# Own terms of a two-way scan moved from VectorE to products in PSUM

## Chip, cores and metric

The kernel runs on one core of one Trainium2 chip. The metric is the device time of one execution in microseconds (us). One execution was taken by the hardware profiler; its span lies inside the device time of the same execution. PE is TensorE, DVE is VectorE, ACT is ScalarE, POOL is GpSimd, SP issues the DMAs.

## The reference, cut to what matters

Four layers work on an image batch `x` of 32 x 192 x 56 x 56 in fp32, each as `x = x + layer(group_norm(x))`: an attention, a two-way linear recurrence (RWKV), a small blur of shifted channels, and a long convolution done by a Fourier transform. Only the second is touched:

```python
def wkv_scan(w, u, k, v):                 # along the 3136 pixels of one image
    def step(carry, kv_t):
        p, q, o = carry                   # o: running maximum, for range only
        kt, vt = kv_t
        no = jnp.maximum(o, u + kt)
        A, Bw = jnp.exp(o - no), jnp.exp(u + kt - no)
        y = (A * p + Bw * vt) / (A * q + Bw)
        no2 = jnp.maximum(w + o, kt)
        A2, B2 = jnp.exp(w + o - no2), jnp.exp(kt - no2)
        return ((A2 * p + B2 * vt, A2 * q + B2, no2), y)
...
```

Without the running maximum this says: with ek = exp(k) and bv = ek v, two sums decay by a factor per pixel and take in bv and ek. The output at a pixel is (p + exp(u) bv) / (q + exp(u) ek), where p and q are the sums of the pixels before. "Own term" is exp(u) times the pixel's own value. The layer does this forwards and backwards, adds both, multiplies by a gate sigmoid(r), normalises over the 192 channels, multiplies by a matrix `Wo` and adds the residual. k, v and r are projections of the normalised x by 192 x 192 matrices. The next layer's group norm needs mean and variance of the result, called x2.

## The kernel before, in words

`all_blocks` runs one layer after the other: `make_filter`, `attention`, `scan_pairs` (the second layer), a guarded version of it that runs only if a value went out of range, and `channel_blocks` (the last two layers). They are separate stages of time.

`scan_pairs` takes the 32 images in 16 pairs. The 192 channels of two images fill three tiles of 128 partitions: tile 0 has channels 0 to 127 of the first image, tile 1 those of the second, tile 2 the last 64 channels of both. Pixels go in four chunks (m) of 784, each in two halves of 392, since a PSUM bank holds 512 fp32 values. A PSUM tile, given by `turned()`, is two banks; there are four of them (`bufs=4`), all of PSUM. `_Pairs.outer` makes one 192 x 192 product for tiles 0 and 1, `_Pairs.inner` for tile 2: per chunk 8 products in `outer` (four with the full 128 x 128 weight `aa`, four that take 64 rows, `ca`) and 6 in `inner` (two full `cc`, four with 64 columns, `ac`).

For one chunk:

- `forwards` normalises x on ACT (L1052), makes k and v on PE, ek = exp(k) on ACT (L1101), bv on DVE (L1106). Then for each tile `scan` and `inverse` run, and DVE multiplies (L1113) into `y`.
- `scan` treats bv (name `p`) and ek (name `q`) alike: POOL copies the carry in (L1065), DVE scans (L1070), POOL copies the new carry out (L1071), and DVE adds the own term with one operation, exp(u) x src + before (L1072), where `before` is the scan's result shifted by one pixel. The buffers `pq` are five.
- `inverse` makes 1 / den on ACT as exp(-ln den) (L1077, L1078); the sum that comes with it is kept in `seen` for the range check.
- `backwards` makes the gate g = 1 / (1 + exp(-r)) from PE and ACT (L1126 to L1131), scans the other way, and DVE multiplies (L1134), adds to `y` (L1135) and multiplies by g (L1136).
- `finish` centres over channels (PE, `centre`), squares on ACT (L1149), takes the variance by a product with `mean_w`, and multiplies by `Wo` (`wog`). DVE scales (L1169), adds bias and residual (L1170), and takes x2's sums with two BATCH_NORM_STATS a tile (`stats_of`, L986). SP stores x2.
- `measure` takes the same statistics of a later pair's x, also at L986. `deviations` and `norm` turn the statistics into mean and scale (small products at L1002 and L1003).

The main loop takes pair p's `backwards` from the last chunk to the first; beside it run `finish` of the chunk before, `forwards` of the next pair, and `measure` of the pair after that. Each engine works its queue strictly in order. The order in each queue is set when the program is built: a scheduler moves instructions of independent work past each other, so queues do not follow the source exactly.

Of the kernel before, what the change touches and what calls it, by code (L numbers as in the profile page):

```python
# [876 lines left out]
def scan_pairs(ctx: ExitStack, tc: tile.TileContext, a, k, x1, x2, rs2, wogT, count):  # L877
# [15 lines left out]
    def small(name, shape):  # L893
        return cp.tile(shape, F32, name=name, tag=name)
# [6 lines left out]
        return [t[:, h * HM : (h + 1) * HM] for h in range(2)]  # L901


    wo = [small("wo_a", [128, C]), small("wo_c", [64, C])]
    lg = [small("lg_a", [128, 1]), small("lg_c", [64, 1])]
    lb = [small("lb_a", [128, 1]), small("lb_c", [64, 1])]
    cen = [small("cen_a", [128, C]), small("cen_c", [64, C])]
    for i, r in enumerate((slice(0, 128), slice(128, C))):
        nc.sync.dma_start(out=wo[i], in_=a["L1_conv_WoT"][r])
        nc.sync.dma_start(out=lg[i], in_=a["L1_conv_ln_g"][r].unsqueeze(1))  # L910
# [10 lines left out]
    for i, r in enumerate((slice(0, 128), slice(128, C))):  # L921
        n = (128, 64)[i]
        ps, _, _ = turned()
        for s in range(2):
            nc.tensor.matmul(ps[:n, 0, :C], cen[s][:, r], wo[s], start=(s == 0), stop=(s == 1))
        turn = wp.tile([128, C], F32, name="turn", tag="turn", bufs=1)
        nc.vector.tensor_copy(turn[:n], ps[:n, 0, :C])
        nc.sync.dma_start(out=wogT[r], in_=turn[:n])

    wk, wv, wr = (blocks(n, a[f"L1_conv_{n}T"]) for n in ("Wk", "Wv", "Wr"))  # L930
    wog, centre, mean_w, group = (
# [2 lines left out]
    wd = pairs.vector("wd", a["L1_conv_w_decay"])  # L934
    eu = pairs.vector("eu", a["L1_conv_u"])
    nc.scalar.activation(eu, eu, AF.Exp)

    w = small("w", [128, 2])
    nc.scalar.activation(w, wd, AF.Exp)
# [64 lines left out]
        pairs.inner(group, [ps[:, 1, 2:3]], [[s] for s in src])  # L1004
        return ps[:, :, 1], ps[:, 1, 2:3]

    def deviations(st):

        mv = moments(st)
        first, third = grouped([mv[:, t, 0:1] for t in range(3)])  # L1010
        mean = sp.tile([128, 3], F32, name="mean", tag="mean", bufs=4)
        nc.vector.tensor_copy(mean[:, 0:2], first)
        nc.vector.tensor_copy(mean[:, 2:3], third)
        d = sp.tile([128, 3], F32, name="d", tag="d", bufs=4)
        nc.vector.tensor_tensor(d, mv[:, :, 0], mean, ALU.subtract)
        nc.vector.tensor_tensor(d, d, d, ALU.mult)
        nc.vector.tensor_tensor(d, d, mv[:, :, 1], ALU.add)
        return mean, d
# [20 lines left out]
    class State:  # L1039


        def __init__(self, p, scaling):
            self.p, (_, self.rs, self.nb) = p, scaling
            self.seen = sp.tile([128, 5, 3 * NM], F32, name="seen", tag="seen", bufs=3)
            self.ek, self.bv, self.y = {}, {}, {}
            self.fore, self.back = start("f"), start("b")
            self.st2 = new_stats("st2")

    def normed(s, m):
        xs = load(s.p, m)  # L1050
# [1 line left out]
            nc.scalar.activation(xs[t], xs[t], AF.Identity, bias=s.nb[:, t : t + 1], scale=s.rs[:, t : t + 1])  # L1052
        return [parts(t) for t in xs]

    def scan(s, m, t, carry, rev):

        b, e = s.bv[m][t], s.ek[m][t]
        c = eu[:, of(t)]
        got = []
        for i, src in enumerate((b, e)):  # L1060
            z = wp.tile([128, MC + 1], F32, name="pq"[i], tag="pq", bufs=5)
            edge, last = (MC, 0) if rev else (0, MC)
            out, before = (z[:, 0:MC], z[:, 1:]) if rev else (z[:, 1:], z[:, 0:MC])
            at = carry[t][i]
            nc.gpsimd.tensor_copy(z[:, edge : edge + 1], at)  # L1065
            if rev:
                out, data = out[:, ::-1], src[:, ::-1]
            else:
                data = src[:, :]
            nc.vector.tensor_tensor_scan(out, decay[:, of(t)].to_broadcast([128, MC]), data, at, ALU.mult, ALU.add)  # L1070
            nc.gpsimd.tensor_copy(at, z[:, last : last + 1])  # L1071
            nc.vector.scalar_tensor_tensor(before, src, c, before, ALU.mult, ALU.add)  # L1072
            got.append(before)
        return got

    def inverse(s, den, m, t, which):
        nc.scalar.activation(den, den, AF.Ln)  # L1077
        nc.scalar.activation(den, den, AF.Exp, scale=-1.0, accum_out=s.seen[:, which, 3 * m + t : 3 * m + t + 1])  # L1078

    def start(way):  # L1080
        carry = [[sp.tile([128, 1], F32, name=f"{way}{i}{t}", tag=f"{way}{i}{t}") for i in range(2)] for t in range(3)]
# [5 lines left out]
    def forwards(s, m):  # L1087
        s.ek[m] = [kp.tile([128, MC], F32, name="ek", tag="ek") for _ in range(3)]
        s.bv[m] = [kp.tile([128, MC], F32, name="bv", tag="bv") for _ in range(3)]
        s.y[m] = [kp.tile([128, MC], F32, name="y", tag="y", bufs=3 * NM + 4) for _ in range(3)]  # L1090
        xn = normed(s, m)
        for tiles in ((0, 1), (2,)):
            for wt in (wk, wv):
                ps = [turned() for _ in tiles]
                if len(tiles) == 2:
                    pairs.outer(wt, [q[2] for q in ps], xn)
                else:
                    pairs.inner(wt, ps[0][2], xn)
                for t, (_, both, _) in zip(tiles, ps):
                    if wt is wk:  # L1100
                        nc.scalar.activation(  # L1101
                            s.ek[m][t].rearrange("p (h n) -> p h n", h=2), both, AF.Exp,
                            accum_out=s.seen[:, 0, 3 * m + t : 3 * m + t + 1],
                        )
                    else:
                        nc.vector.tensor_tensor(  # L1106
                            s.bv[m][t].rearrange("p (h n) -> p h n", h=2), both,
                            s.ek[m][t].rearrange("p (h n) -> p h n", h=2), ALU.mult,
                        )
            for t in tiles:  # L1110
                num, den = scan(s, m, t, s.fore, False)
                inverse(s, den, m, t, 1)
                nc.vector.tensor_tensor(s.y[m][t], num, den, ALU.mult)  # L1113

    def backwards(s, m):
        xn = normed(s, m)
        h = s.y[m]
        for tiles in ((0, 1), (2,)):
            ps = [turned() for _ in tiles]
            if len(tiles) == 2:  # L1120
                pairs.outer(wr, [q[2] for q in ps], xn)
            else:
                pairs.inner(wr, ps[0][2], xn)
            for t, (_, both, _) in zip(tiles, ps):
                g = wp.tile([128, MC], F32, name="g", tag="t")
                nc.scalar.activation(  # L1126
                    g.rearrange("p (h n) -> p h n", h=2), both, AF.Exp, scale=-1.0,
                    accum_out=s.seen[:, 3, 3 * m + t : 3 * m + t + 1],
                )
                nc.scalar.activation(g, g, AF.Ln, bias=1.0)  # L1130
                nc.scalar.activation(g, g, AF.Exp, scale=-1.0)  # L1131
                num, den = scan(s, m, t, s.back, True)
                inverse(s, den, m, t, 2)
                nc.vector.tensor_tensor(num, num, den, ALU.mult)  # L1134
                nc.vector.tensor_tensor(h[t], h[t], num, ALU.add)  # L1135
                nc.vector.tensor_tensor(h[t], h[t], g, ALU.mult)  # L1136

    def finish(s, m):
        h, xs = s.y[m], load(s.p, m)
# [19 lines left out]
        for tiles in ((0, 1), (2,)):  # L1159
            po = [turned() for _ in tiles]  # L1160
            if len(tiles) == 2:
                pairs.outer(wog, [q[2] for q in po], hs)
            else:
                pairs.inner(wog, po[0][2], hs)
            for t, (_, out, _) in zip(tiles, po):
                rd = rds[t]
                rdh = rd.rearrange("p (h n) -> p h n", h=2)
                nc.scalar.activation(rd, rd, AF.Exp, scale=-0.5)
                nc.vector.tensor_tensor(rdh, out, rdh, ALU.mult)  # L1169
                nc.vector.scalar_tensor_tensor(xs[t], rd, cb[:, of(t)], xs[t], ALU.add, ALU.add)  # L1170
                stats_of(s.st2, m, t, xs[t])
        rows = slice(m * MC // S, (m + 1) * MC // S)
        for r, t, i, c in places:
            nc.sync.dma_start(out=x2[c, i, rows, s.p], in_=xs[t][r].rearrange("p (h w) -> p h w", w=S))
# [20 lines left out]
        for t, x in enumerate(load(p, m)):  # L1195
            stats_of(st, m, t, x)

    s, after, before = State(0, norm(*deviations(stats_for(0)))), norm(*deviations(stats_for(1))), None
    for m in range(NM):
        forwards(s, m)  # L1200
    for p in range(last):
        ahead = State(p + 1, after) if p + 1 < last else None
        st = new_stats("st1")
        for i in range(NM):
            m = NM - 1 - i
            backwards(s, m)
            if i > 0:
                finish(s, m + 1)
            elif before is not None:
                finish(before, 0)  # L1210
            if ahead is not None:
                forwards(ahead, i)
            if p + 2 < last:
                if i < 2:
                    measure(st, p + 2, 2 * i)
                    measure(st, p + 2, 2 * i + 1)
                elif i == 2:
                    spread = deviations(st)
                else:
                    after = norm(*spread)  # L1220
            if before is not None:
                if i == 1:
                    before.spread = deviations(before.st2)
                elif i == 2:
                    conclude(before)
        before, s = s, ahead
    finish(before, 0)
    before.spread = deviations(before.st2)
    conclude(before)
    nc.sync.dma_start(out=rs2[0:128], in_=kept_a)  # L1230
    for i, r in enumerate((slice(0, 64), slice(64, 128))):
# [580 lines left out]
```

## Time and profile before

Times are in us; three runs.

| what | value |
|---|---|
| median of the runs (lowest, highest) | 12770.67 (12757.16, 12775.48) |
| profiled execution, device time | 12763.6 |
| its span | 12761.8 |
| mean granted PE clock | 0.953 |
| PE busy in the span | 11522.3 (90%) |
| DVE busy | 11221.3 (88%) |
| ACT busy | 5979.7 (47%) |
| POOL busy | 2199.4 (17%) |
| attention: its last products end | 4996 |
| `scan_pairs`: first projection to last small product | 5081.6 to 8828.5 |

A group of the profile is all instructions of one line, operation and pair of tiles: busy time in all, mean length of one, and the time its engine stood idle just before them. The page divides the span in 40 slices of 319 us; a digit is the busy share in tenths. One fp32 product appears as two matmul records. Records of matmuls overlap, since they are pipelined.

### The profile page before, as it was taken

To read this page: it belongs to the slowest core of one execution; us is meant where nothing else is said; L and a number is where in the kernel's file an instruction comes from. 1 tells how busy PE (TensorE), PEld (TensorE's weight loads), DVE (VectorE), ACT (ScalarE), POOL (GpSimd) and SP (SyncE) were. 2 spreads that over 40 slices of the span, in tenths; PEclk is the share of its full clock that TensorE was granted. 3 is DMA by queue.
4 is the path that set the end of the run, shared out by engine and by line. 5 is a ranking of instruction groups with operands and counts; after the bars stand their busy time and mean duration, and the time that the engine had idled before them with its cause. 6 is when DMAs were issued, how large, how long until landed. Compare 5 with 4: busy or idle time off the path is not lost. (4 is left out here: it accounts for less than half of the span.)

```text
span 12761.8 us, 165194 instructions
## 1 busy us (share of the span) xinstructions
PE 11522.3 (90%) x63158; PEld 7190.8 (56%) x63158; DVE 11221.3 (88%) x15929; ACT 5979.7 (47%) x11146; POOL 2199.4 (17%) x2238
## 2 busy tenths in 40 slices
PE   4999999999999997788878788787999999999999
PEld 1556555565555564333333333334777777777777
DVE  3888888888888886999999999998888888888888
ACT  2554554554554553555555555554333333333333
POOL 0000000000000000544445454544000000000000
PEclk8999999999999998889988899898999999999999
DMA  2111111111111112344443344433111111111111
GB/s 64 40 39 39 39 39 49 47 39 39 39 41 53 41 39 68 84 110 103 99 110 97 105 107 103 103 98 81 43 42 44 42 44 44 42 42 44 43 44 28
DMA packets 949574, 770.40 MB, mean 60 GB/s; under 512 B 769870, under 2 KB 811065, under 8 KB 939760
## 3 DMA queue, kind: packets, MB, share of 16 engines
q1 hardware_dynamic: 948776, 759.74, 22.7%
q8 instruction: 504, 8.26, 0.3%
q14 instruction: 294, 2.41, 0.1%
HBM read 479.96 MB, written 240.50 MB: 56 GB/s over the span
## 5 line engine op out<-in xcount | busy, mean ns | idle before, releaser
L589 DVE SCALAR_TENSOR_TENSOR o<-v_a,dww,o 128x896 f32<-128x896 f32 (+1 forms) x1024 | 1053.0, 1028 | 396.5 <-ACT v_a L563 314.2
L1739 ACT COPY y<-ps 64x252 f32<-64x252 f32 (+1 forms) x2376 | 806.4, 339 | 1132.6 <-PE ps L1733 1102.1
L1657 PE MATMUL ps<-f,real 84*84 84x112 f32 x6144 | 1090.8, 259 | 0.0
L1657 PE MATMUL ps<-f,imag 84*84 84x112 f32 x6144 | 1089.4, 259 | 0.0
L1664 ACT COPY z<-ps 84x448 f32<-84x448 f32 x768 | 405.0, 527 | 1219.9 <-PE ps L1657 1218.4
L1657 PEld LDWEIGHTS ps<-f,real 84*84 84x84 f32 x6144 | 783.9, 153 | 134.3 <-issue 95.8
L1084 POOL MEMSET f<- 128x1 f32 x96 | 8.8, 98 | 4810.6 <-PE ps L739 4805.6
L1077 ACT ACTIVATE q<-q 128x784 f32<-128x784 f32 x384 | 328.9, 857 | 999.1 <-DVE q L1072 753.0
L1657 PEld LDWEIGHTS ps<-f,imag 84*84 84x84 f32 x6144 | 763.8, 153 | 0.0
L606 ACT ACTIVATE pr<-ps,low 98x896 f32<-98x896 f32 (+1 forms) x384 | 351.9, 916 | 838.0 <-DVE low L604 838.0
L602 PE MATMUL ps<-xs_a,gk_a 128*98 128x448 f32 (+1 forms) x1536 | 637.8, 496 | 0.0
L589 DVE SCALAR_TENSOR_TENSOR o<-v_c,dww,o 128x448 f32<-128x448 f32 (+1 forms) x1024 | 634.1, 619 | 4.0
L603 PE MATMUL ps<-xs_c,gk_c 125*98 125x448 f32 (+1 forms) x1536 | 631.9, 492 | 0.0
L694 PE MATMUL ps<-gq_a,xs_a 128*112 128x294 f32 x1792 | 606.2, 419 | 19.2 <-DVE pq L699 19.2
L1674 PE MATMUL ps<-z,f 84*114 84x448 f32 x1536 | 608.9, 539 | 0.0
L695 PE MATMUL ps<-gq_c,xs_c 125*112 125x294 f32 x1792 | 596.4, 414 | 0.0
L1523 POOL TENSOR_TENSOR mat<-tap,tap 114x114 f32<-114x114 f32 x96 | 40.6, 423 | 3163.0 <-PE ps L1583 2310.0
L1631 PE MATMUL re<-y,f 128*84 128x420 f32 (+1 forms) x1152 | 532.0, 542 | 8.7 <-ACT y L1739 7.3
L1631 PE MATMUL im<-y,f 128*84 128x420 f32 (+1 forms) x1152 | 526.8, 538 | 0.0
L1733 PEld LDWEIGHTS ps<-f,padded 114*128 114x128 f32 x3168 | 471.5, 191 | 96.5 <-issue 70.4
L1733 PE MATMUL ps<-f,padded 114*128 114x168 f32 x3168 | 501.9, 310 | 21.4 <-DVE o L1676 10.0
L707 ACT ACTIVATE pq<-pq 112x1176 f32<-112x1176 f32 x224 | 265.3, 1184 | 525.1 <-DVE pq L699 401.9
(358 smaller groups left out, 29470.4 us busy)
## 6 DMA issues: line engine op xcount, KB each, us to landing
x<-x SPq DMA_DIRECT2D x640, 392.0 KB
x<-x SPq DMA_DIRECT2D x640, 196.0 KB
x<-x SPq DMA_DIRECT2D x192, 399.0 KB
out_x<-x SPq DMA_DIRECT2D x384, 196.0 KB
x_a<-in_x SPq DMA_DIRECT2D x32, 1568.0 KB
x<-x_a SPq DMA_DIRECT2D x32, 1568.0 KB
x_c<-in_x SPq DMA_DIRECT2D x64, 392.0 KB
x<-x_c SPq DMA_DIRECT2D x64, 392.0 KB
```

The lines of the kernel that those rows point to most:

```text
L589: nc.vector.scalar_tensor_tensor(dst, tap(i), dww[:, t, i : i + 1], dst, ALU.mult, ALU.add)
L602: mm(ps[P2, h, :n], g[:, cols], xs_a[j][:, px], start=True, stop=False)
L603: mm(ps[P2, h, :n], gk_c[0:KC, 2 * j + h, cols], xs_c[j][0:KC, px], start=False, stop=True)
L606: nc.scalar.activation(pr[:, :, :n], ps[P2, :, :n], AF.Exp, bias=low[:, j, p : p + 1], accum_out=sums[:, j, p : p + 1])
L694: mm(ps[:SUB, i, :HA], xs_a[j][:, px], g, start=True, stop=False)
L695: mm(ps[:SUB, i, :HA], xs_c[j][0:KC, px], gq_c[0:KC, 2 * j + (q + i) // ns], start=False, stop=True)
L1631: nc.tensor.matmul(ps[:, : n * 84], f2[:, i, :], y[:, i0 : i0 + n].rearrange("p g s u -> p (g s u)"), start=True, stop=True)
L1657: nc.tensor.matmul(ps[:84, i * 2 * S : (i + 1) * 2 * S], part[:, i0 + i].rearrange("p s u -> p (s u)"), f3[:, m, :], start=(m == 0), stop= ...
L1664: nc.scalar.copy(z[:, i0 : i0 + n].rearrange("p g m w -> p (g m w)"), ps[:84, : n * 2 * S])
L1674: nc.tensor.matmul(got, f4[:, m, :], z[:, i0 : i0 + n, m, :], start=(m == 0), stop=(m == 1))
L1733: nc.tensor.matmul(ps[:, g * 168 : (g + 1) * 168], flat[:, (g0 + g) * 128 : (g0 + g + 1) * 128], f1, start=True, stop=True)
L1739: nc.scalar.copy(y[64 * m : 64 * m + 64, 2 * g0 + i : 2 * (g0 + n) : 2], got[64 * i : 64 * i + 64, :, :, m, :])
```

## The change

Three things change in `scan_pairs`; the other stages stay.

1. The own term is formed on PE. Two new weights `own` are the identity scaled by exp(u) on the rows, one for tiles 0 and 1, one for tile 2. A scan's numerator and denominator are each the sum in PSUM of `own` x src and `ident` x before. Ln reads the denominator from PSUM, and the multiplications read the numerator from there. The denominator is now done before the numerator.
2. `y` + the backward result is formed in PSUM by two products with `ident`, and the gate multiplies the PSUM value.
3. x2's sums come from an accumulator on the operation that adds the residual, and its squares from an ACT pass with an accumulator, around a value near the mean (the mean of the first finished chunk). `moments_of` puts them together.

In addition the four setup matrices take passing buffers in place of kept ones.

```diff
-    wo = [small("wo_a", [128, C]), small("wo_c", [64, C])]
+    wo = [passing(128), passing(64)]
...
+    ident = small("ident", [128, 128])
+    nc.sync.dma_start(out=ident, in_=k["ident"])
+    own = [small(f"own{i}", [128, 128]) for i in range(2)]
+    for i in range(2):
+        nc.vector.tensor_scalar(own[i], ident, eu[:, i : i + 1], None, ALU.mult)
...
+    def moments_of(s):
+
+        mv = sp.tile([128, 3, 2], F32, name="mv2", tag="mv2")
+        nc.vector.tensor_reduce(mv[:, :, 0], s.sums, AX.X, ALU.add)
+        nc.vector.tensor_reduce(mv[:, :, 1], s.squares, AX.X, ALU.add)
+        nc.vector.tensor_scalar(mv, mv, 1.0 / N, None, ALU.mult)
+        nc.vector.tensor_tensor(s.away, s.away, mv[:, :, 0], ALU.add)
+        nc.vector.tensor_tensor(s.away, s.away, s.away, ALU.mult)
+        nc.vector.tensor_tensor(mv[:, :, 1], mv[:, :, 1], s.away, ALU.subtract)
+        nc.vector.tensor_scalar(mv[:, :, 1], mv[:, :, 1], 0.0, None, ALU.max)
+        return mv
...
-    def scan(s, m, t, carry, rev):
-
-        b, e = s.bv[m][t], s.ek[m][t]
-        c = eu[:, of(t)]
-        got = []
-        for i, src in enumerate((b, e)):
+    def scan(s, m, t, carry, rev, den, which):
+
+        for i, src in ((1, s.ek[m][t]), (0, s.bv[m][t])):
...
             nc.gpsimd.tensor_copy(at, z[:, last : last + 1])
-            nc.vector.scalar_tensor_tensor(before, src, c, before, ALU.mult, ALU.add)
-            got.append(before)
-        return got
-
-    def inverse(s, den, m, t, which):
-        nc.scalar.activation(den, den, AF.Ln)
-        nc.scalar.activation(den, den, AF.Exp, scale=-1.0, accum_out=s.seen[:, which, 3 * m + t : 3 * m + t + 1])
+            _, both, halves = turned()
+            for w, rhs, first in ((own[of(t).start], src, True), (ident, before, False)):
+                for half, part in zip(halves, parts(rhs)):
+                    nc.tensor.matmul(half, w, part, start=first, stop=not first)
+            if i == 1:
+                nc.scalar.activation(den.rearrange("p (h n) -> p h n", h=2), both, AF.Ln)
+                nc.scalar.activation(
+                    den, den, AF.Exp, scale=-1.0, accum_out=s.seen[:, which, 3 * m + t : 3 * m + t + 1]
+                )
+        return both
...
-                num, den = scan(s, m, t, s.fore, False)
-                inverse(s, den, m, t, 1)
-                nc.vector.tensor_tensor(s.y[m][t], num, den, ALU.mult)
+                y = s.y[m][t]
+                num = scan(s, m, t, s.fore, False, y, 1)
+                y = y.rearrange("p (h n) -> p h n", h=2)
+                nc.vector.tensor_tensor(y, num, y, ALU.mult)
...
-                num, den = scan(s, m, t, s.back, True)
-                inverse(s, den, m, t, 2)
-                nc.vector.tensor_tensor(num, num, den, ALU.mult)
-                nc.vector.tensor_tensor(h[t], h[t], num, ALU.add)
-                nc.vector.tensor_tensor(h[t], h[t], g, ALU.mult)
+                den = wp.tile([128, MC], F32, name="den", tag="t")
+                num = scan(s, m, t, s.back, True, den, 2)
+                both = den.rearrange("p (h n) -> p h n", h=2)
+                nc.vector.tensor_tensor(both, num, both, ALU.mult)
+                _, sums, halves = turned()
+                for src, first in ((h[t], True), (den, False)):
+                    for half, part in zip(halves, parts(src)):
+                        nc.tensor.matmul(half, ident, part, start=first, stop=not first)
+                y, g = (u.rearrange("p (h n) -> p h n", h=2) for u in (h[t], g))
+                nc.vector.tensor_tensor(y, sums, g, ALU.mult)
...
-                nc.vector.scalar_tensor_tensor(xs[t], rd, cb[:, of(t)], xs[t], ALU.add, ALU.add)
-                stats_of(s.st2, m, t, xs[t])
+                nc.vector.scalar_tensor_tensor(
+                    xs[t], rd, cb[:, of(t)], xs[t], ALU.add, ALU.add, accum_out=s.sums[:, t, m : m + 1]
+                )
+                if m == NM - 1:
+                    nc.vector.tensor_scalar(
+                        s.away[:, t : t + 1], s.sums[:, t, m : m + 1], -1.0 / MC, None, ALU.mult
+                    )
+                nc.scalar.activation(
+                    rd, xs[t], AF.Square, bias=s.away[:, t : t + 1], accum_out=s.squares[:, t, m : m + 1]
+                )
```

More of the change, by code (lines that the diff above doesn't have):

```diff
@@ L901, in parts, with passing @@
         return [t[:, h * HM : (h + 1) * HM] for h in range(2)]
-    wo = [small("wo_a", [128, C]), small("wo_c", [64, C])]
+    def passing(n):
+        return wp.tile([128, MC], F32, name="passing", tag="t")[:n, :C]
+    wo = [passing(128), passing(64)]
     lg = [small("lg_a", [128, 1]), small("lg_c", [64, 1])]
     lb = [small("lb_a", [128, 1]), small("lb_c", [64, 1])]
-    cen = [small("cen_a", [128, C]), small("cen_c", [64, C])]
+    cen = [passing(128), passing(64)]
     for i, r in enumerate((slice(0, 128), slice(128, C))):
@@ L925, in scan_pairs @@
             nc.tensor.matmul(ps[:n, 0, :C], cen[s][:, r], wo[s], start=(s == 0), stop=(s == 1))
-        turn = wp.tile([128, C], F32, name="turn", tag="turn", bufs=1)
-        nc.vector.tensor_copy(turn[:n], ps[:n, 0, :C])
-        nc.sync.dma_start(out=wogT[r], in_=turn[:n])
+        turn = passing(n)
+        nc.vector.tensor_copy(turn, ps[:n, 0, :C])
+        nc.sync.dma_start(out=wogT[r], in_=turn)
     wk, wv, wr = (blocks(n, a[f"L1_conv_{n}T"]) for n in ("Wk", "Wv", "Wr"))
@@ L1005, in grouped, with deviations @@
         return ps[:, :, 1], ps[:, 1, 2:3]
-    def deviations(st):
-        mv = moments(st)
+    def moments_of(s):
[8 more added lines that the diff above has]
+        return mv
+    def deviations(mv):
         first, third = grouped([mv[:, t, 0:1] for t in range(3)])
@@ L1046, in __init__ @@
             self.fore, self.back = start("f"), start("b")
-            self.st2 = new_stats("st2")
+            self.sums, self.squares = (sp.tile([128, 3, NM], F32, name=n, tag=n, bufs=3) for n in ("sums", "squares"))
+            self.away = sp.tile([128, 3], F32, name="away", tag="away", bufs=3)
     def normed(s, m):
@@ L1196, in measure @@
             stats_of(st, m, t, x)
-    s, after, before = State(0, norm(*deviations(stats_for(0)))), norm(*deviations(stats_for(1))), None
+    s, after, before = State(0, norm(*deviations(moments(stats_for(0))))), norm(*deviations(moments(stats_for(1)))), None
     for m in range(NM):
@@ L1217, in scan_pairs @@
                 elif i == 2:
-                    spread = deviations(st)
+                    spread = deviations(moments(st))
                 else:
@@ L1222, in scan_pairs @@
                 if i == 1:
-                    before.spread = deviations(before.st2)
+                    before.spread = deviations(moments_of(before))
                 elif i == 2:
@@ L1227, in scan_pairs @@
     finish(before, 0)
-    before.spread = deviations(before.st2)
+    before.spread = deviations(moments_of(before))
     conclude(before)
```

## The prediction

> **What bounds the kernel now.** I read the slices of the page first, then the busy time of each engine in the scan stage and, beside it, in a stretch of the last stage (columns: stretch, length, PE, weight loads, DVE, ACT, POOL, granted clock, DMA share, GB/s).
>
> ```profile
> PE   4999999999999997788878788787999999999999
> DVE  3888888888888886999999999998888888888888
> ...
> 5200.00:8600.00 3400.00, 2753.51 (x9818) 1260.42 (x9818) 3342.86 (x3733) 1968.55 (x3254) 1695.00 (x1558) 0.90 0.40 103
> ...
> 10000.00:10500.00 500.00, 494.12 (x3380) 381.62 (x3379) 434.37 (x729) 177.35 (x429) 40.08 (x60) 1.00 0.17 43
> ```
>
> Only slices 16 to 27 are touched by the change. There DVE is busy 3342.86 of 3400 us (98%) and sets the end; PE has 2753.51 (81%), ACT 58%. By the timeline the stage's first projection starts at 5081.6 us and its last small product at 8828.5: 3747 us for 16 pairs x 4 chunks = 64 chunks, 58.5 us a chunk. Next, the groups of that stretch (busy, mean ns | idle before, releaser), of which 58 chunks fall into it (174 tiles / 3):
>
> ```profile
> L1072 DVE SCALAR_TENSOR_TENSOR q<-ek,eu,q 128x784 f32<-128x784 f32 x350 | 357.1, 1024 | 0.1
> L1072 DVE SCALAR_TENSOR_TENSOR p<-bv,eu,p 128x784 f32<-128x784 f32 x348 | 350.3, 1020 | 0.0
> L986 DVE BATCH_NORM_STATS2 st<-x 128x6 f32<-128x392 f32 x684 | 346.5, 554 | 6.2 <-DMA x<-x 6.2
> L1135 DVE TENSOR_TENSOR y<-y,p 128x784 f32<-128x784 f32 x175 | 167.9, 959 | 0.1
> L860 PE MATMUL ps<-x,Wr_aa 128*128 128x392 f32 x464 | 237.6, 665 | 181.3 <-ACT x L1052 176.1 <-DVE bv L1106 5.1
> L863 PE MATMUL ps<-x,Wr_ca 64*128 64x392 f32 x464 | 150.2, 650 | 79.6 <-ACT x L1052 79.5
> L860 PE MATMUL ps<-sq,mean_aa 128*128 128x392 f32 x464 | 221.8, 624 | 146.7 <-ACT sq L1149 145.7
> ```
>
> DVE never waits at these lines; PE does, for ACT. The mean of one matmul (665 ns) is a pipelined latency and no price. The price is the distance between starts, so the third view is PE's timeline (start, length, line, count of records; one fp32 product is two records):
>
> ```profile
> 6542.02 2.90 PE L860 MATMUL ps<-x,Wk_aa 128*128 128x392 f32 x8
> 6544.85 1.59 PE L863 MATMUL ps<-x,Wk_ca 64*128 64x392 f32 x8
> ...
> 6553.32 1.58 PE L870 MATMUL ps<-x,Wk_cc 128*128 128x392 f32 x4
> 6554.84 1.54 PE L873 MATMUL ps<-x,Wk_ac 128*64 128x392 f32 x8
> 6556.30 1.58 PE L870 MATMUL ps<-x,Wv_cc 128*128 128x392 f32 x4
> ...
> 6584.13 5.81 PE L860 MATMUL ps<-sq,mean_aa 128*128 128x392 f32 x8 [6.36 <-ACT sq L1149]
> ...
> 10001.58 3.17 PE L1674 MATMUL ps<-z,f 84*114 84x448 f32 x8
> 10004.59 2.44 PE L1733 MATMUL ps<-f,padded 114*128 114x168 f32 x16
> ```
>
> Four products of 392 columns take 2.83 us (6542.02 to 6544.85), two take 1.52 (6553.32 to 6554.84). In the last stage eight records of 448 columns take 3.01 us (10001.58 to 10004.59), 0.84 ns a column and record; 392 columns make 0.329, a product 0.658 us. So 2.83 is 8 x 0.329 and 0.2 for the change of the array's shape at the run's ends. After a 6.36 us gap the same eight records took 5.81.
>
> **What the change takes from DVE, per chunk of three tiles.** Gone are all L1072 (707.4 us / 58 = 12.2), the addition L1135 (2.9) and half of L986 (x2's sums; 173 / 58 = 3.0): 18.1 of DVE's 57.6 (3342.86 / 58). Operands in PSUM cost no more: L1106 reads PSUM at 963 ns, L1113 SBUF at 961. The accumulator on L1170's form is not in this trace; between nothing and a pass of its own like L986 (2 x 0.55 a tile, 3.3 a chunk), I take 0.2 a tile (ACT's accumulator read, 187 ns). For x2's moments three aggregates of 0.33 a pair go, and some ten small operations of 0.15 to 0.2 come: 0.2 a chunk. DVE then needs about 40 us a chunk.
>
> **ACT** gains three squares of 0.81 (L1149) and accumulator reads of 0.19: 3 us on 33.9 (1968.55 / 58), 37 a chunk. POOL's copies and the 1,280 loads and stores keep their number; the setup adds one 64 KB load and two scalings by eu (0.3 us each by L920). These lie beside longer PE work, and cost nothing as long as PE needs over 40 us.
>
> **What it adds to PE.** Each scan forms numerator and denominator as exp(u) x src plus identity x before, each over two halves: 8 products a tile in `forwards`, 8 in `backwards`, and 4 more for h + den. 20 x 3 = 60 a chunk, 3,840 in all. The built program's PE order has just these 3,840, and the 392-column products of before all remain. They are full 128x128 products in 4-record groups, 30 groups a chunk. A group costs 1.32 us (4 x 0.329) if neighbours share the array's shape, 1.52 if each pays the change. I take 1.32 with 0.2 at each of four blocks: in the run of eight every record has a weight load of its own (464 loads for the 464 records of that line) without that cost, and these groups stand side by side. 30 x 1.32 + 0.6 = 40 us.
>
> What PE does already, from the same rows back to back: Wk, Wv, Wr, centre and wog each 2.83 + 1.52 + 1.52 + 1.46 = 7.33, mean 4.35, statistics 1.8 (four sets of 1.77 a pair at 6559.28, over four chunks, each of two kinds): 42.8. So PE needs 82.8 us a chunk at full clock, against DVE's 40: the bound moves to PE, and 64 x 82.8 = 5299 us replaces 3747.
>
> **Waits.** PE takes its queue in order, so each stall now counts. I followed one chunk through the built orders. Products start when a scan has ended, but the backward scans stand on DVE ahead of the forward chunk's last multiplications, so they are ready; the own terms need no scan; the addition's first product covers the 0.96 us multiplication before its second. The new scans of t = 2 wait for work buffers that PE's products must release (before, DVE's own step released them); a whole forward block lies between. Ln and Exp of one denominator (1.8 us) lie under the numerator's 2.6. The four PSUM buffers turn over in time because each reader follows within 2 us. What remains are late x tiles for Wr: now 255.6 us / 58 = 4.4 a chunk, about 8.8 in every other chunk; the new products of t = 2 stand between Wv and Wr and cover 5.4, which leaves 3.4 in every other chunk, 1.7. The wait for sq (145.7 at the line shown, 30.5 at its second half: 3.0 a chunk) comes from ACT, which stands in its queue at L1077 until DVE's L1072 is through; in the new order Ln waits for PE itself, and ACT reaches the squares with PE still at the centring. I take 2 us a chunk; bounds 0 and 7.4 (both as now).
>
> **The sum.** 64 x (82.8 + 2) = 5427, and 30 for filling the first chunks and the cold clock: 5457. 5457 - 3747 = +1710. The profiled execution took 12763.6 us (span 12761.8), so 14474; the median of the runs is 7 us above it: 14480.
>
> The Trainium skill, "Perfetto Trace Analysis", section Identifying the Most-Contended Engine, says that matmul busy time is a poor measure of TensorE's headroom, and that the share of weight loading should be used. The row gives 1260.42 of 3400 us, 37%. Read so, 120 more loads of 0.19 us make 23 on 22, 45 us a chunk: PE would have room, and the sum would be an estimated 64 x 45 = 2880, 11,900 us in all. That speaks for the change as the busy share does not; here the distances between starts decide, since a load of 0.19 lies hidden under a record of 0.33.
>
> **Rivals.** *The products cost little and DVE's relief shows (faster), 3%.* Place: L1094 after the change. It decides if a product takes under (58.5 - 42.8) / 60 = 0.26 us, for example because an identity has no arithmetic. At 0.1 us: 49 a chunk, 3136, 12,150 us. Against it: attention's identity products (L721, 24 records of 112 columns from 4977.28 to 4979.58, 0.096 each) cost what the filter's dense ones of 112 columns cost (L1657, 0.193 for two).
>
> *The hand-overs stall PE, 17%.* Place: each tile's chain scan, product, Ln, Exp, multiply, sum. If the order's cover fails and each of six tile passes a chunk exposes one multiplication with its hand-over (1.2), and one stall a chunk brings the half clock (3 us by the 5.81 row), or the clock stays at the stage's 0.90: 82.8 + 7.2 + 3 to 82.8 / 0.9 + 7.4, 93 to 99 us; 64 of them are 5952 to 6362, which gives 15,000 to 15,420. For it: clock 0.90 now. Against: it comes from gaps of 6 to 10 us, and a packed PE has 1.00.
>
> *The change doesn't do what it says, 1%*: a limit on `seen` fails and the guarded scan runs as well; thousands of us more. The limits are unchanged, and the values are the same up to rounding.
>
> **How the numbers follow.** Forecast, PE as the bound with few waits: 78%, 14,480. No waits gives 14,350; both old waits 14,825; 1.52 a group adds 64 x 5.4 = 346. The range 14,280 to 15,000 holds these bounds except their worst together, and touches the stall rival. Only the first rival is faster; 1% I leave for a balance between it and the forecast. Faster 0.03, same 0.01, slower 0.96, with 0.2% (26 us) as what a measurement can tell.
>
> **What would show it.** After: DVE's share in the stage near half, PE above 95%, granted clock 0.97 or more; the first stage and the last unchanged; L1094's groups 1.32 us apart (1.52: change of shape is paid); no PE idle over 3 us a chunk except before Wr. I am wrong if PE idles over 10% of the stage, or if a product starts less than 0.6 us after its neighbour.

## The result, and the profile after

The changed kernel takes 14370.73 us (median of four runs, 14357.69 to 14378.54) against 12771.16 before. The ratio is 1.1254, with a 95% interval of 1.1234 to 1.1273: 1600 us slower. The profiled execution took 14373.8 us, 1610 more than that of before, and its stage of the scans runs from the first projection at 5091.2 to the last small product at 10435.0: 5344 us in place of 3747. So 1597 of the 1610 lie in this stage, 83.5 us a chunk in place of 58.5. The stage starts 9.6 us later: attention's last product, in code that is not changed, ends 6.7 later in this execution, and 2.9 are the setup.

The slices of the page after (tenths of busy time, then the granted clock in tenths), and the busy time in three stretches (stretch, length, PE, weight loads, DVE, ACT, POOL, clock, DMA share, GB/s):

```profile
PE   4999999999999989999999999999989999999999
DVE  4888888888888754554554554554478888888888
...
PEclk7999999999999999999999999999999999999999
...
5200.00:10300.00 5100.00, 5070.43 (x17674) 2618.99 (x17672) 2605.48 (x2906) 2314.95 (x3784) 621.75 (x1643) 1.00 0.29 71
...
11000.00:11500.00 500.00, 494.09 (x3371) 380.90 (x3370) 433.04 (x728) 177.35 (x430) 46.63 (x70) 1.00 0.17 42
```

In slices 15 to 28 (counted from 0; a slice is 359 us here) the two rows have changed places: DVE falls to 51% of the stage (2605.48 of 5100), PE rises to 99.4%, at a granted clock of 1.00. The last stage, below it, has the same row as before.

PE's timeline after, in one chunk (start, length, line, records):

```profile
7034.87 1.58 PE L1094 MATMUL ps<-ek,own 128*128 128x392 f32 x4
7036.29 1.48 PE L1094 MATMUL ps<-q,ident 128*128 128x392 f32 x4
7037.61 1.48 PE L1094 MATMUL ps<-bv,own 128*128 128x392 f32 x4
7038.93 1.48 PE L1094 MATMUL ps<-p,ident 128*128 128x392 f32 x4
7040.25 1.48 PE L1162 MATMUL ps<-y,ident 128*128 128x392 f32 x4
7041.56 1.57 PE L1162 MATMUL ps<-den,ident 128*128 128x392 f32 x4
7042.97 1.48 PE L1094 MATMUL ps<-ek,own 128*128 128x392 f32 x4
...
7050.96 1.48 PE L870 MATMUL ps<-x,Wr_cc 128*128 128x392 f32 x4
7052.37 1.54 PE L873 MATMUL ps<-x,Wr_ac 128*64 128x392 f32 x8
```

Starts are 1.32 us apart from group to group, identity or not. Only the first group after another shape of the array takes 1.42; the full-shape projection that follows a block (7050.96) takes 1.41 in place of 1.52. No bracket of idle time stands in these lines. The list of PE's waits over 4400 us of the stage, 53 chunks, has three entries (who waits, at which line, for what: us in all, times, longest):

```profile
PE ps L1094 <- DVE p L1089: 17.5, 21, 1.1
PE ps L1162 <- DVE den L1158: 7.1, 9, 1.4
PE ps L1094 <- DVE bv L1128: 1.7, 4, 0.6
```

That is 26.3 us, 0.5 a chunk. The waits of before, for x and for sq from ACT, are gone. DVE is the one that waits, for PE at its multiplications and for x's loads:

```profile
DVE st L995 <- DMA x<-x: 343.2, 91, 8.5
DVE rd L1197 <- PE ps L863: 256.4, 18, 14.2
DVE den L1158 <- PE ps L1094: 187.8, 72, 4.4
```

(3000 us of the stage.) It costs nothing, since PE has work queued in each of these waits.

### The profile page after: what moved, and what is told of

Same layout as the page of the kernel before. It is cut to its first block, busy times and chain, and to the rows that moved or that the text cites. A ratio compares the mean times of both kernels' runs of the same rounds, so it can differ in the third digit from the quotient of the medians.

```text
span 14372.0 us, 180595 instructions
## 1 busy us (share of the span) xinstructions
PE 13805.4 (96%) x70838; PEld 8552.1 (60%) x70838; DVE 10268.9 (71%) x14891; ACT 6238.3 (43%) x11530; POOL 979.5 (7%) x2238
## 5 line engine op out<-in xcount | busy, mean ns | idle before, releaser
L1094 PE MATMUL ps<-ek,own 128*128 128x392 f32 x1536 | 595.0, 510 | 0.0
L1089 DVE TENSOR_TENSOR_SCAN p<-decay,b,bv 128x784 f32<-128x784 f32 x192 | 353.9, 1843 | 331.6 <-PE ps L1094 331.1
L1094 PE MATMUL ps<-p,ident 128*128 128x392 f32 x1536 | 570.9, 493 | 20.5 <-DVE p L1089 20.4
L995 DVE BATCH_NORM_STATS2 st<-x 128x6 f32<-128x392 f32 x384 | 202.9, 560 | 533.7 <-DMA x<-x 533.6
L1158 DVE TENSOR_TENSOR den<-ps,den 128x784 f32<-128x784 f32 x192 | 186.6, 972 | 539.3 <-PE ps L1094 319.6
L1094 PE MATMUL ps<-bv,own 128*128 128x392 f32 x1536 | 568.6, 493 | 2.0 <-DVE bv L1128 1.7
L1094 PE MATMUL ps<-q,ident 128*128 128x392 f32 x1536 | 568.7, 492 | 0.0
```

The source lines that it names most:

```text
L1094: nc.tensor.matmul(half, w, part, start=first, stop=not first)
```

## The experiments

Each was timed beside the kernel before, and its ratio is to those runs. The two readings to be told apart: *price times count* (the engine with the most work sets the end, here PE's products) and *hand-overs* (one engine waits for another, and the strict order of a queue spreads the wait).

**1. The new sums alone,** on the kernel before:

```diff
-                nc.vector.scalar_tensor_tensor(xs[t], rd, cb[:, of(t)], xs[t], ALU.add, ALU.add)
-                stats_of(s.st2, m, t, xs[t])
+                nc.vector.scalar_tensor_tensor(
+                    xs[t], rd, cb[:, of(t)], xs[t], ALU.add, ALU.add, accum_out=s.sums[:, t, m : m + 1]
+                )
...
+                nc.scalar.activation(
+                    rd, xs[t], AF.Square, bias=s.away[:, t : t + 1], accum_out=s.squares[:, t, m : m + 1]
+                )
...
```

> The kernel before with the third part of the change alone: x2's sums by an accumulator on DVE, its squares on ACT; no product is added on PE. Theory (the engine with the most work per chunk sets the end, and before it is DVE with 57.6 us): DVE loses 3.0 us a chunk (half of the statistics passes) and gains 0.8 (accumulator read 0.2 a tile, small operations 0.2), so 64 x 2.2 = 140 us less: 12630 us. Rival (the relief is given back at once, because ACT, which works strictly in order, does the squares ahead of work that DVE waits for): 12770, and DVE's idle time before a line that waits for ACT grows by as much.

Measured: 12721.57 us against 12760.49, ratio 0.9965 (0.9951 to 0.9979). 39 of the 140 came, somewhat over a quarter. DVE's waits, in 3000 us of the stage, before this edit and with it:

```profile
DVE p L1134 <- ACT q L1078: 34.1, 38, 1.5
DVE rd L1169 <- ACT rd L1168: 9.3, 13, 0.7
```

```profile
DVE p L1146 <- ACT q L1090: 59.4, 52, 2.8
DVE q L1082 <- ACT ek L1113: 57.3, 40, 2.1
```

DVE was busy 2950 of 3000 us and is busy 2869: the relief is there, and most of it turned into waits for ACT, now busy 64% (1921 of 3000) and 58% before. In waits of DVE this is 121 us of 3000 in place of 50, some 90 us over the stage. The rival had the larger part, the theory the sign. It is the one version here that is faster than both kernels, by 0.3%.

**2. The addition alone,** on the kernel before (with the load of `ident` and the passing buffers):

```diff
-                nc.vector.tensor_tensor(h[t], h[t], num, ALU.add)
-                nc.vector.tensor_tensor(h[t], h[t], g, ALU.mult)
+                _, sums, halves = turned()
+                for src, first in ((h[t], True), (num, False)):
+                    for half, part in zip(halves, parts(src)):
+                        nc.tensor.matmul(half, ident, part, start=first, stop=not first)
+                y, g = (u.rearrange("p (h n) -> p h n", h=2) for u in (h[t], g))
+                nc.vector.tensor_tensor(y, sums, g, ALU.mult)
```

> The kernel before with the second part alone: y and the backward result are added by 12 products a chunk with the identity, own terms and statistics stay on DVE. Theory: DVE loses 2.9 us a chunk, PE rises from 42.8 to 42.8 + 6 x 1.32 = 50.7 us a chunk, still under DVE's 54.7, so 64 x 2.9 = 186 us less: 12585 us. Rival (the hand-over costs: DVE must wait for PE between its multiplication and the gate): 12770 to 12900, with idle time on DVE before the gate's line, released by PE.

Measured: 13203.17 us, ratio 1.0348 (1.0331 to 1.0365), 443 slower, though neither engine is full: in 3000 us PE is busy 2713 and DVE 2548. The theory is wrong here. DVE's waits, PE's waits at the addition (L1143), PE's timeline of one chunk, and DVE's first line behind it:

```profile
DVE rd L1178 <- PE ps L863: 176.1, 35, 6.3
DVE y L1145 <- PE ps L1143: 140.8, 80, 3.9
DVE st L991 <- DMA x<-x: 118.2, 34, 4.2
...
PE ps L1143 <- DVE p L1139: 48.0, 64, 2.9
PE ps L1143 <- ACT g L1131: 38.3, 12, 4.0
...
PE ps L1143 <- DVE bv L1111: 36.6, 23, 2.9
```

```profile
6596.91 2.98 PE L1143 MATMUL ps<-y,ident 128*128 128x392 f32 x4 [3.99 <-ACT g L1131]
...
6608.53 1.59 PE L1143 MATMUL ps<-p,ident 128*128 128x392 f32 x4 [0.33 <-DVE p L1139]
6609.95 1.48 PE L860 MATMUL ps<-y,cen_aa 128*128 128x392 f32 x4
...
6615.67 1.58 PE L1143 MATMUL ps<-p,ident 128*128 128x392 f32 x4 [0.42 <-DVE p L1139]
6617.19 1.53 PE L873 MATMUL ps<-y,cen_ac 128*64 128x392 f32 x6
6618.65 1.58 PE L860 MATMUL ps<-sq,mean_aa 128*128 128x392 f32 x4
6620.07 1.48 PE L1143 MATMUL ps<-p,ident 128*128 128x392 f32 x4
6621.39 1.48 PE L860 MATMUL ps<-sq,mean_aa 128*128 128x392 f32 x4
...
6624.31 2.90 PE L860 MATMUL ps<-y,wog_aa 128*128 128x392 f32 x8
...
6628.83 1.86 DVE L1178 TENSOR_TENSOR rd<-ps,rd 128x784 f32<-128x784 f32 x2 [6.27 <-PE ps L863]
```

The additions stand in PE's queue among `finish`'s centring and mean, and wog stands behind them all. PE works through them from 6608.53 with one wait of 0.42 us, but DVE, whose backward chain is done, idles 6.27 us at L1178 until wog is there. Of the 122.9 us that PE waits at the additions, 48.0 are for DVE's multiplications. The other 74.9 are for g and bv, which read other PSUM tiles; the first product of an addition (`y`,`ident`) needs neither of them, so there it seems to wait until one of the four PSUM tiles is free. That the addition costs its place among these four is a rival to the order of the queue, and no run here takes them apart.

**3. The changed kernel with the old sums** (part three undone: `stats_of` after the addition of the residual, no squares):

```diff
...
-                nc.scalar.activation(
-                    rd, xs[t], AF.Square, bias=s.away[:, t : t + 1], accum_out=s.squares[:, t, m : m + 1]
-                )
...
+                stats_of(s.st2, m, t, xs[t])
```

> The changed kernel with the third part undone: x2's statistics are DVE's two passes a tile again, ACT has no squares. Theory (PE's 82 to 83 us of products a chunk set the end and all else is hidden): 14370 us within 30, though DVE gets 2.2 us a chunk more and ACT 3 less. Rival (the chain between the engines sets the end): 64 x 2.2 = 140 us more, 14510, or less than 14300 if ACT's squares were in the way.

Measured: 14425.26 us, ratio 1.1298 (1.1279 to 1.1317), 55 above the changed kernel by the medians (0.4%); the two intervals do not overlap, and the slowest run of the changed kernel, 14378.54, is below the fastest here, 14409.39. That is outside the theory's 30 us, but nearer to it than to either side of the rival: not quite all else is hidden. PE is busy 98.7% (4935.62 of 5000) in place of 99.4%. Its waits over the whole stage are 72 us in place of 36, two thirds of the 55; those for DVE's bv are 18.5 us in 4400, and 1.7 in the changed kernel.

**4. The changed kernel with the addition on DVE:**

```diff
-                _, sums, halves = turned()
-                for src, first in ((h[t], True), (den, False)):
-                    for half, part in zip(halves, parts(src)):
-                        nc.tensor.matmul(half, ident, part, start=first, stop=not first)
...
+                nc.vector.tensor_tensor(h[t], h[t], den, ALU.add)
+                nc.vector.tensor_tensor(h[t], h[t], g, ALU.mult)
```

> The changed kernel with the second part undone: DVE adds y and the backward result, so 6 groups of PE records a chunk are gone (24 products of 30 groups' 120 records; own terms stay on PE). Theory (price times count on PE): 64 x 6 x 1.32 = 507 us less, 13865 us, with PE still over 98% busy in the stage. Rival (PE's waits at the hand-overs were a part of the time): more than 600 less, below 13770, or under 400 less, if DVE's extra 2.9 us a chunk come onto the chain.

Measured: 13891.84 us, ratio 1.0884 (1.0866 to 1.0902): 479 below the changed kernel, where 507 were expected. 479 / 64 / 6 is 1.25 us a group; PE is busy 98.6% of the stage (4438.53 of 4500). The missing 28 us are waits: PE's are 68 us over the stage in place of 36 (for DVE's p and bv), and with these 32 us added a group comes to 1.33. All six groups are products with the identity, so these are not cheaper. The expectation's bracket miscounted: 6 groups are 12 products, 24 records.

**5. Own terms in 16 bits** (`own`, the scans' results, ek and bv take bfloat16 tiles as well):

```diff
+    short = cp.tile([128, 128], mybir.dt.bfloat16, name="short", tag="short")
+    nc.vector.tensor_copy(short, ident)
...
-            for w, rhs, first in ((own[of(t).start], src, True), (ident, before, False)):
+            for w, rhs, first in ((own[of(t).start], src, True), (short, before, False)):
```

> The changed kernel with ek, bv, the scans' results, own and the identity of the own terms in 16 bits (bfloat16): it rounds these values, so its output is less exact, and only the 48 own-term products a chunk change, from two records of 0.329 us each in fp32 to one short one; the addition stays in fp32. Theory (price times count on PE): if a 16-bit product takes a quarter of 0.658, PE needs 82.8 - 48 x 0.49 = 59 us a chunk, 64 x 23.7 = 1517 less than 14371: 12850 us, if PE stays fed; with waits as in the kernel with the addition alone (7 us a chunk) 13300. Rival (the hand-overs between the engines hold the time, not the products): above 13800.

Measured: 13425.26 us, ratio 1.0513 (1.0495 to 1.0530), 946 below the changed kernel. The price fell as expected; PE's timeline:

```profile
7015.13 0.51 PE L1096 MATMUL ps<-ek,own 128*128 128x392 bf16 x2
7015.47 0.50 PE L1096 MATMUL ps<-q,short 128*128 128x392 bf16 x2
7015.81 0.49 PE L1096 MATMUL ps<-bv,own 128*128 128x392 bf16 x2
...
7020.18 0.49 PE L1096 MATMUL ps<-bv,own 128*128 128x392 bf16 x2 [1.56 <-ACT g L1151]
```

Two products now take 0.34 us in place of 1.32. But PE is no longer packed: busy 90.6% (3442.92 of 3800), at a clock of 0.95. The time lies between the two expectations, 125 us above the theory's figure with waits and 375 below the rival. Of the 1517, 946 came. PE's waits are 417 us over the stage in place of 36, which is 381 of the 571 that did not come; about 190 more are busy time of PE beyond the sum. So the price is most of the loss, and once PE has room, waits come back.

**6. Three of twelve own terms on PE** (forward denominators; the new sums stay, the addition is DVE's, the denominator is still done before the numerator):

```diff
+            if not (i == 1 and not rev):
+                nc.vector.scalar_tensor_tensor(before, src, eu[:, of(t)], before, ALU.mult, ALU.add)
+                both = before.rearrange("p (h n) -> p h n", h=2)
+            else:
+                _, both, halves = turned()
```

> The changed kernel with only the own terms of the forward denominators on PE (3 of 12 a chunk, 12 products); the other nine and the addition are DVE's again, x2's sums stay as changed. Theory (the engine with the most work per chunk): against the kernel with the new sums alone (12722) DVE loses 3 x 1.02 us a chunk and PE has 42.8 + 6 x 1.32 = 50.7: 64 x 3.05 = 195 less, 12525 us. Rival (PE works strictly in order, so products that wait for a scan hold up the projections behind them, as the addition alone did): 12850 to 13200, with DVE idle before lines that wait for PE.

Measured: 12929.74 us, ratio 1.0126 (1.0109 to 1.0143). That is 208 more than the new sums alone, where 195 less were expected. The rival: in 3000 us PE is busy 2684 and DVE 2581, PE waits 144.6 us at L1098 for DVE's scan, and DVE 148.1 for finish's products at L1197.

**7. The addition alone, `finish` written ahead of `backwards`:**

```diff
-            backwards(s, m)
             if i > 0:
                 finish(s, m + 1)
             elif before is not None:
                 finish(before, 0)
+            backwards(s, m)
```

> The kernel with the addition alone on PE (13203 us), with finish of the chunk before written ahead of backwards, so that finish's products need not stand behind additions that wait for DVE. Theory (head of line: the 443 us were lost because finish's projections queued behind the additions, and DVE then waited 3.8 us a chunk at its scaling of PSUM and 2.6 for x): most of these come back, 12600 to 12900. Rival (the addition's own hand-over, 3.1 us a chunk at the gate's line, and its price make the loss): 13100 or more.

Measured: 12885.26 us, ratio 1.0089 (1.0073 to 1.0106), 318 better than experiment 2. DVE's wait at its scaling of finish's PSUM is no longer among its longest; the gate's wait for PE falls from 140.8 to 22.5 us in 3000, and of PE's waits at the additions those for g and bv are gone and 41.3 us for the multiplication are left. Experiment 9 gives the control.

**8. Six of twelve own terms** (`if not (i == 1)` in the edit of 6: all denominators):

> The changed kernel with the own terms of all denominators on PE (6 of 12 a chunk, 24 products), numerators and addition on DVE, x2's sums as changed. Theory: PE 42.8 + 12 x 1.32 + 0.6 = 59.2 us a chunk, DVE about 57 - 6.1 = 51, so PE is the bound: 64 x 59.2 = 3790 in place of 3747, 12810 us, and up to 3 us of waits a chunk more, 13000. Rival (waits in PE's queue decide): above 13200.

Measured: 13196.60 us, ratio 1.0334 (1.0317 to 1.0351). That is 197 above the theory with its waits and 3 us short of the rival. The larger part of the excess of 387 over 12810 is waiting: PE waits 263 us over the stage, in 3000 us of it 193.3 for the scan at L1098; it is busy 2806 of these 3000, at a clock of 0.95.

**9. The order alone:** the edit of 7 on the kernel before.

> The kernel before, with finish of the chunk before written ahead of backwards and nothing else: the control for the addition with finish first (12885 us). Theory (DVE is busy 98% and sets the end, the place of finish's products on PE is covered): 12770 us within 40, so that 115 of the 443 us of the addition remain as its own hand-over and 318 were the queue. Rival (the new order alone is faster or slower by more than 100 us): then the gain there was the order's own and says nothing on the queue.

Measured: 12890.72 us, ratio 1.0093 (1.0076 to 1.0110). The theory's "covered" is wrong: the order by itself costs 126 us, DVE waits 80.5 us of 3000 for ek from ACT, and PE 283.0 for the normalised x. Against this control the addition costs nothing (12885 and 12891, overlapping intervals), against 443 in the old order. So the order makes its loss; but the 186 us of DVE's relief that were expected do not come either. The edit reorders all engines' queues, so that PE's is the one that matters is argued from the waits and not shown. With both edits DVE is busy 2743 of 3000 us, with the order alone 2887: of the difference, two thirds became waits for ACT (196.7 us in place of 100.6), the rest waits for x's loads and for PE.

**10. Experiment 6 with `finish` first.**

> The kernel with only the forward denominators' own terms on PE and the new sums (12930 us), with finish first. Theory (head of line): DVE's 148 us of 3000 at its scaling of finish's PSUM go, about 3 us a chunk, 190 in all: 12740 us; PE's wait for the scan at the identity's products stays. Rival (the wait is at the products themselves): 12880 or more.

Measured: 13277.05 us, ratio 1.0399 (1.0382 to 1.0416), worse by 347 than experiment 6, and by 315 than its own control, experiment 12. DVE's wait at finish's PSUM did not go: it is 324.3 us of 3000. PE waits 371.8 for the normalised x; but it does so in experiment 12 too (378.9), where DVE has no such wait, so why it grew is not shown. Here the reading by the head of the queue did not hold as a recipe.

**11. The backward denominators in their place** (`i == 1 and rev`), `finish` first.

> As the forward denominators with finish first, but the three own terms moved are the backward ones, where the scans stand ahead in DVE's queue. Theory: with nothing late on PE, DVE's 3.05 us a chunk are gained over the new sums alone: 12722 - 195 = 12530 us. Rival (PE is held by a scan here too): 12750 or more.

Measured: 12789.04 us, ratio 1.0020 (1.0010 to 1.0029), 67 above the new sums alone. But the order costs by itself, and the control for it is experiment 12, the new sums with `finish` first: against its 12961.97 these three own terms on PE gain 173 us, where 195 were expected. The rival's mechanism is not there: PE's list of waits has no entry for a scan, and its wait for the normalised x is 6.1 us of 3000 in place of 378.9. DVE waits 154.6 us for 1 / den from ACT and 82.7 for PE. The denominator comes first here and the numerator there; that difference was not tried apart.

**12. The new sums alone with `finish` first.**

> The kernel with the new sums alone (12722 us) with finish first. Theory: ACT's squares lie earlier against the next exponentials, so the 59 + 57 us of 3000 that DVE waits for ACT (2.3 a chunk) shrink: 12600 to 12722 us. Rival (the order adds waits, as DVE's 102 us for ek in the addition with finish first): 12750 or more.

Measured: 12961.97 us, ratio 1.0149 (1.0132 to 1.0166): the rival. DVE waits 147.5 us of 3000 for ek and 88.5 for 1 / den.

## Why the prediction was right, point by point

- *PE becomes the bound.* Shown: 99.4% busy, DVE 51%, and in experiments 4 and 5 the time follows PE's products.
- *The price of a group, 1.32 us.* Measured 1.32 in the timeline, and 1.25 from experiment 4, 1.33 with its new waits taken out. The bound of 1.52, with a change of shape for each group, does not apply.
- *82.8 us of PE work a chunk.* Measured 83.5 in all, of which 0.5 are waits: 83.0. Behind this agreement stand small errors of both signs: four blocks at 0.2 are 0.8 and not 0.6; a change of shape cost 0.1 at a block's first group (1.42) and not 0.2; and some 20 us of the stage, 0.3 a chunk, went to products at a lower clock, which the sum does not have (last section).
- *2 us of waits.* Over-sized, measured 0.5. Of this term, the 1.7 for late x tiles fell away: PE's list of waits has no entry for x, presumably because the loads have 25 us more time a chunk. The 30 us for filling were too much as well: over 13 pairs in the middle of the stage a chunk takes 83.5 us as well, and 64 of these are all of the 5344. Together, less 13 us for the 83.0, these make the forecast 110 us too high (1710 against 1600).
- *DVE about 40 us, ACT 37.* By their shares of 83.5: 42.7 and 37.9. The accumulator on DVE was taken at 0.2 a tile; it is a `DVE_READ_ACCUMULATOR` of 0.08. The relief of 18.1 was added up from lengths, which the prediction itself calls no price for PE. On a full DVE they are none either (two rows of the timeline before):

```profile
6516.18 1.03 DVE L1072 SCALAR_TENSOR_TENSOR p<-bv,eu,p 128x784 f32<-128x784 f32 x1
6517.13 1.03 DVE L1072 SCALAR_TENSOR_TENSOR q<-ek,eu,q 128x784 f32<-128x784 f32 x1
```

  Starts are 0.95 us apart. With such distances (0.88 for L1135, 0.47 for L986) the relief is about 16.8, and DVE's need 41.6. As PE was the bound by far, this cost the forecast nothing.
- *The clock.* 1.00 in the stage, 0.90 before, as the packed last stage had it. That the half clock comes from gaps of 6 to 10 us is not the whole of it (last section).
- *The share of weight loading.* It is one of two measures that the Trainium skill, "Perfetto Trace Analysis", Identifying the Most-Contended Engine, names for TensorE's headroom. Here it is 2618.99 of 5100 us, 51%, which reads as half free. PE was full. The distances between starts decided rightly.
- *The rival "products cost little"* falls with experiment 4: the identity's products have the full price.
- *The rival "hand-overs stall PE"* is wrong for the changed kernel, where PE's own work covers them. Waits between the engines do decide versions in between: experiments 2, 6 and 8 are 3.5%, 1.3% and 3.3% slower than the kernel before, with room on both engines, and the sums by engine in their expectations missed them by 390 to 620 us. Experiment 11 against 12 is the exception, where the sum nearly held. So the sum came out for the changed kernel because one engine is far over the others, 83 us against 43.

Open: why `finish` first costs 126 us by itself is read only from the waits (ACT's order), and was not tried apart; nor was an order of PE's queue set by hand, or another number of PSUM tiles.

## What to carry to other kernels

Moving elementwise work to the matrix engine is a trade at a price: here one DVE operation, 0.95 us from start to start, became four fp32 products, 2.63 us of PE, and PE had 15 us a chunk to spare, not 40. Read the spare time of an engine from the distance between starts, and multiply by the count. Where both engines stay under their limit, the sum by engine is not enough: the addition cost 443 us in one program order and nothing in another. And a version needs a control in its own order: against the wrong one, experiment 11 looks like a loss of 67 us, against the right one it gains 173.

## What the hardware showed that I had not expected

PE's granted clock can fall without an idle gap. Two sets of small products for the statistics (one column each) stand one after the other in front of Wr once in a pair. The timeline after, the last of them and the projection behind, and the row of the projection's 4.53 us (the clock is its third number from the end):

```profile
7114.26 0.38 PE L870 MATMUL ps<-d,grp_cc 128*128 128x1 f32 x2
7114.57 0.28 PE L873 MATMUL ps<-d,grp_ac 128*64 128x1 f32 x4
7114.78 4.59 PE L860 MATMUL ps<-x,Wr_aa 128*128 128x392 f32 x8
7119.31 1.59 PE L863 MATMUL ps<-x,Wr_ca 64*128 64x392 f32 x8
```

```profile
7114.78:7119.31 4.53, 4.53 (x13) 2.25 (x9) 2.38 (x9) 0.41 (x2) 0.28 (x2) 0.62 0.00 0
```

The small products follow each other from 7111.35 to 7114.78 without a wait, and the eight records after them take 4.53 us in place of 2.83, at a granted clock of 0.62; before and after it is 1.00. This was so in 10 of 13 such places (clock 0.50 to 0.64, 4.35 to 5.53 us). At the other three, and behind each single set of 1.7 us, the eight took 2.83. Why three escape, no run shows.

POOL's carry copies of one column took far longer before, with DVE busy 98%, than in the changed kernel. The group that differs most, before and after (here 182 of its 192 copies), in that order:

```profile
L1071 POOL COPY b<-p 128x1 f32<-128x1 f32 x192 | 329.2, 1714 | 265.3 <-DVE p L1070 194.8 <-DVE d L1015 35.8 <-DVE d L1016 28.5
```

```profile
L1090 POOL COPY b<-p 128x1 f32<-128x1 f32 x182 | 33.4, 183 | 117.4 <-DVE p L1089 107.9 <-DVE seen L1223 1.8 <-POOL p L1084 0.3
```

The other three groups of the copy out fell as well, but not to that: from 1548, 1456 and 1267 ns to 629, 1170 and 651. The four groups of copies in took 625 to 1199 ns and take 181 to 183. All copies have the same size, so the longer times are not the copy's own work; what holds them back was not tried apart, and lengths on POOL are rough.
